# A graph layer's gathers and sums: loads moved to ScalarE's queue, one-hot tiles built earlier, three PSUM buffers for sums, and empty steps behind a pack's stores

## The chip, the cores and the metric

The kernel runs on one core of a Trainium2 chip. The metric is the device time of one launch in microseconds (us); a kernel's time is the median of several runs. One execution is also taken by the profiler, and everything that is said of lines, waits and engines comes from that one.

The core has TensorE (PE in the profile; PEld is its loading of weights), VectorE (DVE), ScalarE (ACT), GpSimd (POOL) and SyncE (SP). Each has its own queue and takes its instructions in order; they wait for one another through semaphores. SP does nothing here but issue DMAs, and ScalarE and GpSimd can issue them as well.

## What is computed

A graph layer on 50,000 nodes of 160 numbers and 1,650,000 edges, sorted by destination. Each edge sends a message that is linear in its source's row and in the edge's four numbers; the messages are added up by destination, go through another linear map and a relu, are added to x twice, and a layer norm over the 160 numbers ends it.

```python
s = x[:, :MUL0]
v = x[:, MUL0:].reshape(n, MUL1, 3)
ss, vv = (s[src], v[src])
e0 = sh[:, 0:1]
e1 = sh[:, 1:4]
dot = jnp.einsum('eui,ei->eu', vv, e1)
out0 = C0 * (ss * e0 @ W1 + dot * INV3 @ W2)
p3 = (ss @ W3)[:, :, None] * e1[:, None, :] * INV3
p4 = jnp.einsum('eui,uw->ewi', vv * e0[:, :, None], W4) * INV3
p5 = jnp.einsum('eui,uw->ewi', jnp.cross(vv, e1[:, None, :]), W5) * INV6
out1 = C1 * (p3 + p4 + p5)
m = jnp.concatenate([out0, out1.reshape(-1, 3 * MUL1)], axis=1)
m_agg = jax.ops.segment_sum(m, dst, num_segments=n)
hs = m_agg[:, :MUL0] @ Ws * LIN_S
hv = jnp.einsum('nui,uw->nwi', m_agg[:, MUL0:].reshape(n, MUL1, 3), Wv) * LIN_V
h = jnp.concatenate([hs, hv.reshape(n, 3 * MUL1)], axis=1)
...
x = _layernorm(x + x + jax.nn.relu(h), axis=-1)
```

(The last line puts together what two functions of the reference do.)

## The kernel before

The order of the two linear steps is turned round: the kernel first adds up, for each node, the gathered rows weighted by each of the edge's four numbers (4 x 160 sums per node), and then multiplies these sums by one matrix that joins all the weights.

**Edges.** A unit is 128 edges, a group is 6 units whose destinations lie in 32 neighbouring nodes, and a *pair* is two groups: 12 units. There are 1,044 pairs, and the main loop (line 853) runs over them. For a pair p:

- `gather` (L345): 12 indirect DMAs on GpSimd (L349), each bringing 128 rows of x (640 bytes apiece) into the tile `xg`. That pool (`rows`) has 4 buffers, so the first gather of pair p waits for the last matmul of pair p-4.
- `spread` (L354), on VectorE: `hot` (L358) is 1 where an edge's destination is one of the 32 nodes, and `ha` (L361) is `hot` times the edge's four numbers, 128 columns per unit.
- `group_sums` (L381): 12 matmuls on TensorE (L386), `ha` against `xg`, into `ps`, a PSUM tile of 2 x 160 columns from a pool of 2 buffers (`psA`). They are fp32 and run in two passes, so the profile has 25,044 of them. It is a generator that gives control back after each matmul.
- `turn_sums` (L394), on VectorE: a transpose of `ps` into `sums` (L398) and two additions into the `ring` (L405), the running sums of a stretch of nodes.

**Nodes.** 391 blocks of 128 nodes. When no later group touches a block, tasks are put into a queue that `work` (L748) draws from after each of the 12 matmuls of a pair: `do_ahead` (the load of `xt`, rows of x for two blocks, L644), 2 pairs later `do_block` (five matmuls of the ring with the joined weights into `phb`, L704, then `y`, `st` and `mv` on VectorE, L182 to L186), 3 pairs later `do_root` (`rstd` by ScalarE, L191), 4 pairs later `do_store` (reciprocal L195 and `o` L196 on VectorE), 6 pairs later `do_send` (`out`, L784, for two blocks). `phb` comes from the pool `psM` of 2 buffers.

**Edges' data.** Every 10 pairs `load` (L250) brings the next 20 groups' indices and numbers; `do_place` makes the tiles of indices (`si`), of places (`rel`) and of the edges' numbers (`pk`, in PSUM) from it, starting with `first` on VectorE (L318) and a small matmul into `bank` (L320). A first part of the edges is read as it is. The rest is first packed by the kernel itself: each node's edge to itself is taken out of the lists, the rest closed up.

**Packs.** 16 packs of 128 long rows of edges, one after another, each over some 63 pairs. `pack` (L463) gives a list of steps, some of them empty (`None`): a read (L474 to L478), 59 steps of work on ScalarE and VectorE (L482 to L584) and empty ones, then 17 `store` steps, in each of which SP issues up to 16 DMAs to places that it reads from a table (L618): a row of `edges` and a row of `selves` for each of 8 rows. The loop (L872 to L881) spreads the steps evenly over the pairs between one pack's end and the next one's due pair. `load` then reads `edges`, and `ask_own` (L661) reads `selves` (`sr`) and the rows of x (`xr`, L675) for two blocks at a time, 6 pairs before their segment's first pair; `set_own` puts them into the ring.

**Queues.** SP issues all loads, all results and all stores, in program order: `dq = nc.sync`. ScalarE computes `rstd` and the packs' casts and issues a few loads at the start. GpSimd issues only gathers. The order within each queue is the program's order (a manual schedule, L851). The order of TensorE's and VectorE's work in a pair is set by the j at which the loop does things:

```python
for j, ps in enumerate(group_sums(p, rows, has.pop(p))):
    if j == 1 and turning:
        turn_sums(*turning)
        turning = None
    if j == 3 and p + 1 < len(pairs):
        s1, g1, ng1 = pairs[p + 1]
        has[p + 1] = spread(placed[s1], (g1 - s1 * SG) * G, ng1 * G)
    work(1.0)
```

`turning` is the pair before, so VectorE turns pair p-1 and then builds `ha` of pair p+1.

Of the kernel before, what the change touches and what calls it, by code (L numbers as in the profile page):

```python
# [50 lines left out]
P = 128  # L51
# [22 lines left out]
RP = 128  # L74
RS = 16
KM = 31

def plan(n_nodes, n_edges):

# [23 lines left out]
def tile_gnn_resnorm(ctx: ExitStack, tc: tile.TileContext, x, src, dst, attr, W1, W2, W3, W4, W5, Ws, Wv, out, n_edges):  # L103
# [123 lines left out]
    with tc.tile_pool(name="once", bufs=1) as once, tc.tile_pool(name="raw", bufs=2) as rawp, \  # L227
# [2 lines left out]
            tc.tile_pool(name="ring", bufs=2) as ringp, tc.tile_pool(name="node", bufs=3) as np_, \  # L230
            tc.tile_pool(name="ahead", bufs=4) as aheadp, tc.tile_pool(name="outs", bufs=3) as outp, \
            tc.tile_pool(name="psC", bufs=1, space=PSUM) as psC, tc.tile_pool(name="psK", bufs=2, space=PSUM) as psK, \
            tc.tile_pool(name="psP", bufs=1, space=PSUM) as psP, tc.tile_pool(name="psA", bufs=2, space=PSUM) as psA, \
            tc.tile_pool(name="psM", bufs=2, space=PSUM) as psM, ExitStack() as later_pools:

        spotp, ownp = (later_pools.enter_context(tc.tile_pool(name=name, bufs=bufs))
                       for name, bufs in (("spot", 3), ("own", 2)))
# [6 lines left out]
        slotsP = bank[:, 0, :]  # L244
        nc.vector.tensor_copy(slotsP, slots)

        dq = nc.sync
        begun = []

        def load(s):  # L250

            g0 = s * SG
            n = (min(NG, g0 + SG) - g0) * G
            if g0 >= NH:
                p0 = g0 * G * P - EH
                r6 = rawp.tile([P, P, 2 + NK], F32, name="r6")
                dq.dma_start(r6[:n].rearrange("u p c -> u (p c)"),
                             edges[0, p0 * (2 + NK):(p0 + n * P) * (2 + NK)].rearrange("(u q) -> u q", u=n))
                return s, n, None, r6[:n, :, 0], r6[:n, :, 1], r6[:n, :, 2:]
            e = slice(g0 * G * P, (g0 * G + n) * P)  # L260
            ri = rawp.tile([P, 2, P], I32, name="ri")
            ra = rawp.tile([P, P, NK], F32, name="ra")
            dq.dma_start(ri[:n, 0, :], src1[e].rearrange("(u p) o -> u (p o)", p=P))
            dq.dma_start(ri[:n, 1, :], dst1[e].rearrange("(u p) o -> u (p o)", p=P))
            dq.dma_start(ra[:n].rearrange("u p k -> u (p k)"), attr[e].rearrange("(u p) k -> u (p k)", p=P))
            return s, n, ri, None, None, ra[:n]

        def cast(loaded):
# [102 lines left out]
        def fresh(kind):  # L371
            written[kind].append([])

        def wrote(kind, ins):
            ws = written[kind]
            for old in ws[-3] if len(ws) > 2 else []:
                tc.declare_no_dep(ins.ins, old, reason="its reader has waited for it")
            ws[-1].append(ins.ins)
            return ins

        def group_sums(p, rows, ha):  # L381

            ps = psA.tile([P, PG, D], F32, name="ps")
            fresh("ps")
            for j, xr in enumerate(rows):
                mm = nc.tensor.matmul(ps[:, j // G, :], ha[:, j].rearrange("p k w -> p (k w)"), xr,  # L386
                                      start=j % G == 0, stop=j % G == G - 1)
                if j % G == 0:
                    wrote("ps", mm)
                else:  # L390
                    written["ps"][-1].append(mm.ins)
                yield ps
# [70 lines left out]
        def pack(c):  # L463
# [7 lines left out]
            def read():  # L471
                T["pri"] = pri = packp.tile([P, 2, L + 1], I32, name="pri")
                T["pra"] = pra = packp.tile([P, LW, NK], F32, name="pra")
                dq.dma_start(pri[:n, 0, :L], src1[e].rearrange("(r e) o -> r (e o)", e=L))  # L474
                dq.dma_start(pri[:n, 1, :L], dst1[e].rearrange("(r e) o -> r (e o)", e=L))

                dq.dma_start(pri[:n, 1, L:], dst1[e0 + L:e0 + L + n * L].rearrange("(r e) o -> r (e o)", e=L)[:, 0:1])
                dq.dma_start(pra[:n, :L].rearrange("r e k -> r (e k)"), attr[e].rearrange("(r e) k -> r (e k)", e=L))  # L478

            def begin():  # L480
                T["prow"] = rows = packp.tile([P, L + 1, C], F32, name="prow")
# [142 lines left out]


            for head, j in [(False, j) for j in range(RS)] + [(True, 0)]:
                steps.append(partial(store, head, j))
            return steps + [stored]

        def rows_of(b):  # L630
            nb = min(P, N - b * P)
# [2 lines left out]
        def together(b):  # L634

            bs = list(range(b // BP * BP, min(nblocks, b // BP * BP + BP)))
            return bs if all(rows_of(i)[0] == P for i in bs) else [b]

        def ahead(bs):

            nb = rows_of(bs[0])[0]
            n0, n1 = rows_of(bs[0])[1].start, rows_of(bs[-1])[1].stop
            xt = aheadp.tile([P, BP, D], F32, name="xt")
            dq.dma_start(xt[:nb, :len(bs)], x[n0:n1, :].rearrange("(h n) d -> n h d", h=len(bs)))  # L644

            return [(xt[:, h],) for h in range(len(bs))]

# [13 lines left out]
        def ask_own(k, bs, got):  # L661

            n0, n1 = rows_of(bs[0])[1].start, rows_of(bs[-1])[1].stop
            assert rows_stored[0] == NR or row_start(rows_stored[0])[1][0] >= n1
            n = n1 - n0
            nq = next(q for q in range(math.ceil(n / W), n + 1) if n % q == 0)
            m = n // nq
            assert nq <= BP * P // W
            xr = ownp.tile([P, BP * P // W, D], F32, name="xr")
            sr = ownp.tile([P, BP * P // W], F32, name="sr")  # L670
            xs = x[n0:n1, :].rearrange("(w q) d -> w (q d)", q=nq).unsqueeze(0).to_broadcast([NK, m, nq * D])
            ss = selves[0, n0 * NK:n1 * NK].rearrange("(w q k) -> k w q", q=nq, k=NK)
            with nc.allow_non_contiguous_dma(reason="one number of each node"):
                if m == W:
                    dq.dma_start(xr[:, :nq].rearrange("p q d -> p (q d)"), xs)  # L675
                    dq.dma_start(sr[:, :nq], ss)
                else:
                    nc.vector.memset(xr[:, :nq], 0.0)
                    nc.vector.memset(sr[:, :nq], 0.0)
                    for k_ in range(NK):  # L680
                        r = slice(k_ * W, k_ * W + m)
                        dq.dma_start(xr[r, :nq].rearrange("p q d -> p (q d)"), xs[k_])
                        dq.dma_start(sr[r, :nq], ss[k_])
            got.extend((xr, sr, nq))

        def set_own(k, bs, got):
# [8 lines left out]
            if c0 + nq * W < c1:  # L695
                nc.vector.memset(ring[k][:, :, c0 + nq * W:c1], 0.0)

        def block(b, xt):
            nb, row = rows_of(b)
            k, c0 = b // SB, b % SB * P  # L700
            ph = psM.tile([P, D], F32, name="phb", tag="misc")
            fresh("misc")
            for i in range(ND):
                wrote("misc", nc.tensor.matmul(ph[:nb], ring[k][:, i, c0:c0 + nb], BWk[:, i, :],  # L704
                                               start=i == 0, stop=i == ND - 1))
                yield 1
            return norm1(np_, ph[:nb], xt[:nb], nb)
# [33 lines left out]
        def after_pair(p, f, *args):  # L741
            later.setdefault(p, []).append((f, args))
# [15 lines left out]
                else:  # L758
                    credit[0] -= cost

        of_nodes, resid, rstds, outs = {}, {}, {}, {}

        def do_ahead(b):
            bs = together(b)
# [1 line left out]
                of_nodes.update(zip(bs, ahead(bs)))  # L766

        def do_block(b):
            resid[b] = yield from block(b, *of_nodes.pop(b))

        def do_root(b):
            rstds[b] = norm2(np_, resid[b][1], rows_of(b)[0])
# [7 lines left out]
        def do_send(b):  # L780
            bs = together(b)
            if b == bs[-1]:
                n0, n1 = rows_of(bs[0])[1].start, rows_of(b)[1].stop
                dq.dma_start(out[n0:n1, :].rearrange("(h n) d -> n h d", h=len(bs)),  # L784
                             outs.pop(bs[0])[:rows_of(b)[0], :len(bs)])

        def do_cast(s):
# [57 lines left out]
                after_pair(p - 2, set_own, k, bs, got)  # L845
        for b, g in enumerate(last_of):
            p = g // PG
            after_pair(max(p, START - 1), do_ahead, b)
            for d, f in ((2, do_block), (3, do_root), (4, do_store), (6, do_send)):
                after_pair(p + d, f, b)  # L850
        later_pools.enter_context(tc.manual_schedule(engines={ET.SP, ET.PE, ET.DVE, ET.Activation}))  # L851
        turning = None
        for p, (s, g, ng) in enumerate(pairs):
# [8 lines left out]
                    after_pair(p + 8, read_flags)  # L862
            rows = gather(placed[s], (g - s * SG) * G, ng * G)
            for j, ps in enumerate(group_sums(p, rows, has.pop(p))):
                if j == 1 and turning:
                    turn_sums(*turning)
                    turning = None
                if j == 3 and p + 1 < len(pairs):
                    s1, g1, ng1 = pairs[p + 1]
                    has[p + 1] = spread(placed[s1], (g1 - s1 * SG) * G, ng1 * G)  # L870
                work(1.0)
                if packs and p >= START:  # L872
                    when = p + (j + 1) / (ng * G)
                    todo = math.ceil(len(packs[0]) * min(1, (when - began) / max(1, due[0] - began)))
                    for step in packs[0][done:todo]:
                        if step:
                            step()
                    done = max(done, todo)
                    if done == len(packs[0]):
                        packs.pop(0), due.pop(0)  # L880
                        done, began = 0, when  # L881
# [174 lines left out]
```

## Time and profile before

| what | value |
|---|---|
| median of 10 runs | 17,998.04 us (17,987.92 to 18,016.4) |
| the profiled execution: time of the run | 17,988.15 us |
| its span in the profile | 17,986.0 us |
| TensorE's granted clock, mean | 0.625 |
| DMA traffic | 1,337 MB, 74 GB/s over the span |
| gathers' share of the 16 DMA engines' time | 24.2% |
| one gather on GpSimd (L349), shortest / median / longest | 940 / 946 / 4,777 ns |
| transposes of `sums` (L398) | 529.3 us busy, 5,996.5 us idle before them |
| `y` (L182) | 125.7 us busy, 3,784.8 us idle before |
| additions into the ring (L405) | 683.0 us busy |

Busy time is the time in which an engine runs instructions; issuing DMAs, waiting on semaphores and branches don't count. "Idle before" is the time that an engine did nothing just ahead of the instructions of a line, with what ended it; "remote" there means a releaser that the trace doesn't show, and "issue" means that nothing was waited for as far as the profile shows. In the list of waits a line reads: engine and line, what it waited for, total, number of times, longest.

### The profile page before, as it was taken

The numbers are of one execution on the slowest core, as the hardware profiler recorded it, in microseconds if no ns is written. First come the engines' busy times: TensorE is split into PE (matmuls) and PEld (weight loads), VectorE is DVE, ScalarE is ACT, GpSimd is POOL, SyncE is SP. The second block draws the span as 40 slices with busy tenths as digits, with TensorE's granted clock in tenths as the row PEclk, the third lists the DMA queues.
The fourth block names the chain that finished last, engine by engine and source line by source line (L and its number), as shares of the span: only waits on it lengthen the run. The fifth ranks groups of instructions, "written<-read, shape, count | busy, mean of one in ns | idle before, by whom it ended". The sixth has DMA issues, their size and how long they took to land. (4 is left out here: it accounts for less than half of the span.)

```text
span 17986.0 us, 99721 instructions
## 1 busy us (share of the span) xinstructions
PE 6903.9 (38%) x29811; PEld 6018.3 (33%) x29812; DVE 7033.1 (39%) x11269; ACT 228.2 (1%) x479; POOL 12110.3 (67%) x12535
## 2 busy tenths in 40 slices
PE   3333333333333333333333333334333333334334
PEld 3333333333333333333333333333333333333333
DVE  4343443434434343443433434344343433434332
ACT  0000000000000000000000000000000000000000
POOL 6666666666666666666666666666666666666666
PEclk6666666666666666666666666666666666666666
DMA  2222323233232322323223233332323223233322
GB/s 71 75 69 72 80 70 81 69 81 72 71 81 70 83 69 73 80 69 83 72 71 80 70 79 73 79 73 72 81 70 82 69 73 80 69 81 72 73 72 63
DMA packets 961715, 1337.18 MB, mean 74 GB/s; under 512 B 411739, under 2 KB 716048, under 8 KB 957182
## 3 DMA queue, kind: packets, MB, share of 16 engines
q0 software_dynamic: 601056, 1026.60, 24.2%
q1 hardware_dynamic: 358674, 302.87, 6.1%
q8 instruction: 238, 3.90, 0.1%
q14 instruction: 307, 2.51, 0.0%
q10 hardware_dynamic: 1440, 1.29, 0.0%
HBM read 1258.50 MB, written 71.40 MB: 74 GB/s over the span
## 5 line engine op out<-in xcount | busy, mean ns | idle before, releaser
L349 POOL DMA_INDIRECT xg<-in_x,si x12522 | 12106.6, 967 | 5854.0 <-issue 3663.0
L386 PE MATMUL ps<-xg,ha 128*128 128x160 f32 x25044 | 6279.1, 383 | 9065.1 <-issue 8170.0
L386 PEld LDWEIGHTS ps<-xg,ha 128*128 128x128 f32 x25044 | 5181.9, 254 | 9865.6 <-issue 8903.4
L398 DVE STREAM_TRANSPOSE sums<-ps 128x320 f32<-128x320 f32 x1044 | 529.3, 507 | 5996.5 <-remote 3768.2
L361 DVE TENSOR_TENSOR ha<-hot,pk 128x1536 f32<-128x1536 f32 x1044 | 1830.4, 1753 | 35.8
L182 DVE SCALAR_TENSOR_TENSOR y<-phb,xt 128x160 f32<-128x160 f32 x391 | 125.7, 321 | 3784.8 <-PE ps L386 1817.9
L704 PE MATMUL phb<-BWk,ring 128*128 128x160 f32 (+1 forms) x3910 | 1177.8, 386 | 464.1 <-issue 462.7
L704 PEld LDWEIGHTS phb<-BWk,ring 128*128 128x128 f32 (+1 forms) x3910 | 917.0, 263 | 477.4 <-issue 476.6
L405 DVE TENSOR_TENSOR ring<-ring,sums 128x160 f32 x2087 | 683.0, 327 | 310.5 <-issue 220.1
L358 DVE TENSOR_TENSOR hot<-bank,rel 128x384 f32<-128x384 f32 x1044 | 572.8, 549 | 137.8 <-remote 91.6
L693 DVE STREAM_TRANSPOSE ring<-xr 128x1280 f32<-128x1280 f32 x188 | 465.9, 2478 | 6.5
L566 DVE COPY_PREDICATED prow<-marks,prow 128x2370 f32<-128x2370 int32 (+8 forms) x160 | 445.3, 2783 | 1.1
L320 PE MATMUL bank<-first,ones 120*128 120x20 f32 (+1 forms) x210 | 57.8, 357 | 769.6 <-DVE first L318 506.0
L191 ACT ACTIVATE rstd<-mv,eps_t 128x1 f32<-128x1 f32 x391 | 115.2, 295 | 17028.1 <-DVE st L184 5280.4
L320 PEld LDWEIGHTS bank<-first,ones 120*128 120x128 f32 (+1 forms) x210 | 49.0, 287 | 808.0 <-DVE first L318 529.0
L326 PE MATMUL bank<-ident,r 120*128 120x120 f32 x100 | 46.5, 465 | 702.8 <-DVE baseB L322 401.1
L566 DVE COPY_PREDICATED pra<-marks,pra 128x1580 f32<-128x1580 int32 (+8 forms) x160 | 306.8, 1917 | 0.0
L689 DVE TENSOR_TENSOR xr<-xr,sr 128x1280 f32<-128x1280 f32 x188 | 277.0, 1474 | 57.1 <-DMA sr<-selves 32.7
L326 PEld LDWEIGHTS bank<-ident,r 120*128 120x128 f32 x100 | 21.1, 211 | 727.0 <-DVE baseB L322 414.9
L196 DVE TENSOR_SCALAR o<-y,mv,rstd 128x160 f32<-128x160 f32 x391 | 147.3, 377 | 18.9 <-remote 2.9
L402 DVE TENSOR_TENSOR ring<-ring 128x1280 f32<-128x1280 f32 x97 | 142.8, 1473 | 1.8
L331 PE MATMUL pk<-ident,r 120*128 120x120 f32 (+1 forms) x400 | 140.0, 401 | 0.0
(349 smaller groups left out, 2157.5 us busy)
## 6 DMA issues: line engine op xcount, KB each, us to landing
xg<-in_x,si POOLq DMA_INDIRECT x12522
xr<-in_x SPq DMA_DIRECT2D x187, 640.0 KB
edges<-prow SPq DMA_DIRECT2D x1994, 18.5 KB
r<-edges SPq DMA_DIRECT2D x99, 360.0 KB
selves<-mine SPq DMA_DIRECT2D x1992, 0.5 KB
xt<-in_x SPq DMA_DIRECT2D x195, 160.0 KB
out<-o SPq DMA_DIRECT2D x195, 160.0 KB
pra<-in_attr SPq DMA_DIRECT2D x15, 1580.0 KB
```

The lines of the kernel that those rows point to most:

```text
L196: nc.vector.tensor_scalar(o[:n], y[:n], mv[:n, 0:1], rstd[:n], op0=ALU.subtract, op1=ALU.mult)
L349: nc.gpsimd.indirect_dma_start(out=xg[:, j, :], out_offset=None, in_=x, in_offset=bass.IndirectOffsetOnAxis(ap=placed[0][:, u + j:u + j + ...
L358: nc.vector.tensor_tensor(hot[:, :n], slotsP[:, 0:W].unsqueeze(1).to_broadcast([P, n, W]), rel[:, u:u + n].unsqueeze(2).to_broadcast([P, n ...
L361: nc.vector.tensor_tensor(ha[:, :n], hot[:, :n].unsqueeze(2).to_broadcast([P, n, NK, W]), pk[:, :, u:u + n].rearrange("p k u -> p u k").un ...
L386: mm = nc.tensor.matmul(ps[:, j // G, :], ha[:, j].rearrange("p k w -> p (k w)"), xr, start=j % G == 0, stop=j % G == G - 1)
L398: nc.vector.transpose(at[:, :ng], ps[:, :ng].rearrange("p g (b f) -> p g b f", f=FB))
L402: nc.vector.tensor_tensor(ring[k][:, :, :TW - S], ring[k][:, :, :TW - S], ring[k - 1][:, :, S:], op=ALU.add)
L405: nc.vector.tensor_tensor(here, here, at[:, i], op=ALU.add)
L566: nc.vector.copy_predicated(what[:n, a:e], mi[:, r].unsqueeze(2).to_broadcast([n, e - a, what.shape[2]]), what[:n, a + d:e + d])
L689: nc.vector.tensor_tensor(xr[:, :nq], xr[:, :nq], sr[:, :nq].unsqueeze(2).to_broadcast([P, nq, D]), op=ALU.mult)
L693: nc.vector.transpose(ring[k][:, :, c0:c0 + nq * W].rearrange("p b (w q) -> p q b w", q=nq), xr[:, :nq].rearrange("p q (b f) -> p q b f", ...
L704: wrote("misc", nc.tensor.matmul(ph[:nb], ring[k][:, i, c0:c0 + nb], BWk[:, i, :], start=i == 0, stop=i == ND - 1))
```

## The change

- `load` (but for the very first), the packs' reads, `xt`, `xr` and `sr`, and the results `out` are issued by ScalarE (`loads = nc.scalar`). The stores stay on SP.
- `xt` is asked for 3 pairs earlier.
- `ha` of pair p+1 is built at j == 0, ahead of the turn of pair p-1, which stays at j == 1.
- The pool of `ps` has 3 buffers, that of `phb` one, whose tile holds two blocks and is taken at the first of the two. `wrote` declares away the order between a `ps` tile's matmuls and those of the tile whose buffer it takes over, now the fourth last; for the others nothing is declared any more.
- In a pack each store step is followed by an empty one, and the end of the pack by 70 empty ones: 164 steps, where there were 77, spread over the same pairs.

```diff
+REST = 70
...
-            tc.tile_pool(name="psP", bufs=1, space=PSUM) as psP, tc.tile_pool(name="psA", bufs=2, space=PSUM) as psA, \
-            tc.tile_pool(name="psM", bufs=2, space=PSUM) as psM, ExitStack() as later_pools:
+            tc.tile_pool(name="psP", bufs=1, space=PSUM) as psP, tc.tile_pool(name="psA", bufs=3, space=PSUM) as psA, \
+            tc.tile_pool(name="psM", bufs=1, space=PSUM) as psM, ExitStack() as later_pools:
...
-        dq = nc.sync
+        dq, loads = nc.sync, nc.scalar
...
         def load(s):
 
+            q = loads if s else dq
...
-                dq.dma_start(r6[:n].rearrange("u p c -> u (p c)"),
+                q.dma_start(r6[:n].rearrange("u p c -> u (p c)"),
...
         def wrote(kind, ins):
             ws = written[kind]
-            for old in ws[-3] if len(ws) > 2 else []:
+            for old in ws[-4] if kind == "ps" and len(ws) > 3 else []:
                 tc.declare_no_dep(ins.ins, old, reason="its reader has waited for it")
...
-                dq.dma_start(pri[:n, 0, :L], src1[e].rearrange("(r e) o -> r (e o)", e=L))
+                loads.dma_start(pri[:n, 0, :L], src1[e].rearrange("(r e) o -> r (e o)", e=L))
...
             for head, j in [(False, j) for j in range(RS)] + [(True, 0)]:
-                steps.append(partial(store, head, j))
-            return steps + [stored]
+                steps += [partial(store, head, j), None]
+            return steps + [stored] + [None] * REST
...
-            dq.dma_start(xt[:nb, :len(bs)], x[n0:n1, :].rearrange("(h n) d -> n h d", h=len(bs)))
+            loads.dma_start(xt[:nb, :len(bs)], x[n0:n1, :].rearrange("(h n) d -> n h d", h=len(bs)))
...
-                    dq.dma_start(xr[:, :nq].rearrange("p q d -> p (q d)"), xs)
-                    dq.dma_start(sr[:, :nq], ss)
+                    loads.dma_start(xr[:, :nq].rearrange("p q d -> p (q d)"), xs)
+                    loads.dma_start(sr[:, :nq], ss)
...
-        def block(b, xt):
+        def block(b, xt, ph):
             nb, row = rows_of(b)
             k, c0 = b // SB, b % SB * P
-            ph = psM.tile([P, D], F32, name="phb", tag="misc")
-            fresh("misc")
...
         def do_block(b):
-            resid[b] = yield from block(b, *of_nodes.pop(b))
+            bs = together(b)
+            if b == bs[0]:
+                sums_of[b] = psM.tile([P, BP, D], F32, name="phb", tag="misc")
+                fresh("misc")
+            resid[b] = yield from block(b, *of_nodes.pop(b), sums_of[bs[0]][:, b - bs[0]])
...
-                dq.dma_start(out[n0:n1, :].rearrange("(h n) d -> n h d", h=len(bs)),
+                loads.dma_start(out[n0:n1, :].rearrange("(h n) d -> n h d", h=len(bs)),
                              outs.pop(bs[0])[:rows_of(b)[0], :len(bs)])
...
-            after_pair(max(p, START - 1), do_ahead, b)
+            after_pair(max(p - 3, START - 1), do_ahead, b)
...
             for j, ps in enumerate(group_sums(p, rows, has.pop(p))):
+                if j == 0 and p + 1 < len(pairs):
+                    s1, g1, ng1 = pairs[p + 1]
+                    has[p + 1] = spread(placed[s1], (g1 - s1 * SG) * G, ng1 * G)
                 if j == 1 and turning:
                     turn_sums(*turning)
                     turning = None
-                if j == 3 and p + 1 < len(pairs):
-                    s1, g1, ng1 = pairs[p + 1]
-                    has[p + 1] = spread(placed[s1], (g1 - s1 * SG) * G, ng1 * G)
                 work(1.0)
```

More of the change, by code (lines that the diff above doesn't have):

```diff
@@ L262, in load @@
             ra = rawp.tile([P, P, NK], F32, name="ra")
-            dq.dma_start(ri[:n, 0, :], src1[e].rearrange("(u p) o -> u (p o)", p=P))
-            dq.dma_start(ri[:n, 1, :], dst1[e].rearrange("(u p) o -> u (p o)", p=P))
-            dq.dma_start(ra[:n].rearrange("u p k -> u (p k)"), attr[e].rearrange("(u p) k -> u (p k)", p=P))
+            q.dma_start(ri[:n, 0, :], src1[e].rearrange("(u p) o -> u (p o)", p=P))
+            q.dma_start(ri[:n, 1, :], dst1[e].rearrange("(u p) o -> u (p o)", p=P))
+            q.dma_start(ra[:n].rearrange("u p k -> u (p k)"), attr[e].rearrange("(u p) k -> u (p k)", p=P))
             return s, n, ri, None, None, ra[:n]
@@ L473, in read @@
                 T["pra"] = pra = packp.tile([P, LW, NK], F32, name="pra")
-                dq.dma_start(pri[:n, 0, :L], src1[e].rearrange("(r e) o -> r (e o)", e=L))
-                dq.dma_start(pri[:n, 1, :L], dst1[e].rearrange("(r e) o -> r (e o)", e=L))
-                dq.dma_start(pri[:n, 1, L:], dst1[e0 + L:e0 + L + n * L].rearrange("(r e) o -> r (e o)", e=L)[:, 0:1])
-                dq.dma_start(pra[:n, :L].rearrange("r e k -> r (e k)"), attr[e].rearrange("(r e) k -> r (e k)", e=L))
+                loads.dma_start(pri[:n, 0, :L], src1[e].rearrange("(r e) o -> r (e o)", e=L))
+                loads.dma_start(pri[:n, 1, :L], dst1[e].rearrange("(r e) o -> r (e o)", e=L))
+                loads.dma_start(pri[:n, 1, L:], dst1[e0 + L:e0 + L + n * L].rearrange("(r e) o -> r (e o)", e=L)[:, 0:1])
+                loads.dma_start(pra[:n, :L].rearrange("r e k -> r (e k)"), attr[e].rearrange("(r e) k -> r (e k)", e=L))
             def begin():
@@ L681, in ask_own @@
                         r = slice(k_ * W, k_ * W + m)
-                        dq.dma_start(xr[r, :nq].rearrange("p q d -> p (q d)"), xs[k_])
-                        dq.dma_start(sr[r, :nq], ss[k_])
+                        loads.dma_start(xr[r, :nq].rearrange("p q d -> p (q d)"), xs[k_])
+                        loads.dma_start(sr[r, :nq], ss[k_])
             got.extend((xr, sr, nq))
@@ L759, in work @@
                     credit[0] -= cost
-        of_nodes, resid, rstds, outs = {}, {}, {}, {}
+        of_nodes, resid, rstds, outs, sums_of = {}, {}, {}, {}, {}
         def do_ahead(b):
```

## The prediction

> **What bounds the kernel now.** I read the engines' busy times first, then the list of waits, then the groups of instructions, then one stretch of the timeline. The waits of GpSimd (POOL):
>
> ```profile
> span 17986.0 us, 99721 instructions
> PE 6903.9 (38%) x29811; PEld 6018.3 (33%) x29812; DVE 7033.1 (39%) x11269; ACT 228.2 (1%) x479; POOL 12110.3 (67%) x12535
> ...
> POOL xg L349 <- issue: 3663.0, 12005, 1.8
> POOL xg L349 <- PE ps L386: 1176.2, 224, 46.8
> POOL xg L349 <- remote: 929.2, 231, 7.7
> POOL xg L349 <- PE phb L704: 63.9, 11, 7.6
> ```
>
> The columns of the last four lines are total idle us, times, longest. GpSimd issues 12,522 gathers. They are busy 12,106.6 us (third block below) and 3,663.0 us lie between them as issue, 0.305 us apiece, for which nothing else is to blame. Its whole idle time before L349 is 5,854.0, so 5,854.0 - 3,663.0 = 2,191 us are real waits, nearly all of them for TensorE to free a gather buffer (the three rows above are 2,169 us in 466 waits, 4.65 us each). 12,106.6 + 3,663.0 + 2,191 = 17,961, and some 25 us of start and tail make the span. No other engine is over 39% busy. So the floor of this kernel is near 15,800 us (17,986 - 2,191), and everything turns on the 2,191.
>
> Why is TensorE late? The rows of the groups, and the other engines' waits:
>
> ```profile
> L349 POOL DMA_INDIRECT xg<-in_x,si x12522 | 12106.6, 967 | 5854.0 <-issue 3663.0
> L386 PE MATMUL ps<-xg,ha 128*128 128x160 f32 x25044 | 6279.1, 383 | 9065.1 <-issue 8170.0
> L361 DVE TENSOR_TENSOR ha<-hot,pk 128x1536 f32<-128x1536 f32 x1044 | 1830.4, 1753 | 35.8
> ...
> DVE sums L398 <- remote: 3768.2, 278, 42.1
> DVE y L182 <- PE ps L386: 1817.9, 129, 34.5
> DVE y L182 <- DMA xt<-in_x: 233.5, 7, 93.3
> ```
>
> L386 is idle 9,065 us and 8,170 of them are "issue": the profile sees nothing that it waits for. The timeline shows it; start, duration, then idle time before in brackets:
>
> ```profile
> 9002.57 0.42 PE L386 MATMUL ps<-xg,ha 128*128 128x160 f32 x1 [2.38 <-issue]
> 9005.37 0.43 PE L386 MATMUL ps<-xg,ha 128*128 128x160 f32 x1 [2.37 <-issue]
> 9008.17 0.43 PE L386 MATMUL ps<-xg,ha 128*128 128x160 f32 x1 [2.37 <-issue]
> 9010.99 0.32 DVE L182 SCALAR_TENSOR_TENSOR y<-phb,xt 128x160 f32<-128x160 f32 x1 [30.14 <-PE ps L386]
> 9012.20 0.94 POOL L349 DMA_INDIRECT xg<-in_x,si  x1 [6.04 <-PE ps L386]
> 9018.02 5.97 PE L386 MATMUL ps<-xg,ha 128*128 128x160 f32 x24 [4.33 <-issue]
> ```
>
> TensorE creeps, one half-matmul (fp32 takes two) each 2.8 us, until GpSimd has stood still for some microseconds; then VectorE's wait ends too, and TensorE does 24 in 5.97 us. About half of the span (9,186 us in 358 stretches) is such creeping. I counted from the trace's instruction times what goes with it. At the start of 331 of 419 stalls of GpSimd over 1 us, TensorE was creeping (its last matmul under 3 us before); at 88 it stood. A stall's mean length by the pairs of groups since the last stall is 3.64 us (1 pair), 4.46 (2), 5.92 (3), 6.16 (4): about 2 us per pair, however the stalls fall. So something passes TensorE's instructions at a nearly fixed rate while gathers are issued, and a stall is where it catches up. Of what nature it is the trace doesn't tell.
>
> **The change, part by part.**
>
> *Loads and results to ScalarE.* Some 950 DMA issues leave SP for ScalarE, 228.2 us busy. At 0.4 to 0.7 us each (timeline: `out` 0.40, `xt` 0.46) that is 400 to 650 us on an idle engine; on the path they cost nothing. What they save is waiting behind SP's stores: 17 store steps per pack of 16 stores each. The 93.3 us above is `xt` queued behind pack 0's stores; VectorE, then TensorE, then GpSimd stood, the 46.8 us. Only one other long stall leads to a late load: 10.0 us at 10,652, a pack's read that came late (ScalarE 54.7 us on `pri`, VectorE 33.1 behind it). Seven near 11.5 us have another cause (TensorE stands at the group start L320 for VectorE's `first`, which stands behind `y`, which waits for TensorE's notice), and the change leaves that order alone. Gain: (46.8 - 4.65) + (10.0 - 4.65) = 47 us. Bounds: 0, if new waits take their place, to 94, if every stall above 8 us falls back to 4.65 (nine, 136 us in all, less 9 x 4.65). I take 47. `xt` (195 issues), asked for 3 pairs earlier, is in the same sum.
>
> The Trainium skill ("Trainium Kernel Development and Optimization", Key Constraints) speaks against this part: queues of several engines run on the same DMA engines, so splitting them saves only the issuing engine's time. By it alone the part is worth 0. The profile has 233.5 us of waits for `xt`, which were issue order, not transfer.
>
> What is now queued behind them: `rstd` (L191) on ScalarE, and behind it the reciprocal (L195) at the head of VectorE's queue. The second `xr` issue of a segment held SP 12 to 18 us (15.66 at 813.55). The cover: ScalarE waits for `st`, `mv`, `y` 14,363 us in all (44.5 us of it in this stretch of the timeline), so these issues mostly end before VectorE reaches the block. `out` waits for `o` there too, but the `rstd` behind it needs still later work of VectorE. The cover is thin: `rstd` was ready 15.2 us (median) before the reciprocal, under 8 in a quarter of 391 cases. Taken at 0; priced in rival B.
>
> *`ha` before the turn.* No instruction is added; hot and ha (0.549 + 1.753 us) now stand before the turn of pair p-1, not behind it. In before a turn that waits for TensorE's notice holds back the next `ha`, for which TensorE then waits. I counted 43 stalls that begin in that state, 5.6 us each. Bounds: 0 (the 2 us per pair are only paid later) to 43 x 5.6 = 240 us. Between: the stall comes one pair later, at 3.5 pairs rather than 2.5. By the lengths above that is (4.46 + 5.92)/2 / 2.5 = 2.08 against (5.92 + 6.16)/2 / 3.5 = 1.73 us per pair, over 43 x 3.5 = 150 pairs: 53 us. I take 53, since the rows by length speak for it.
>
> *Three buffers for `ps`, one for `phb` (for two blocks).* TensorE's first matmul of a pair now needs the turn of p-3, not p-2. While it creeps, no buffer holds it, so I take 0; the upper bound is in rival A. The Trainium skill ("Perfetto Trace Analysis", Optimizing Strategies) would have independent groups change PSUM banks so that reading out overlaps matmuls; by it this gains what TensorE waits for `ps`, which the 331 of 419 above leave small. With one `phb` the first matmul of the next two blocks waits for `y`: in before `y` ended 22 us (median) ahead of the next block's first matmul, and later than it in 2 of 390. 0 to 2 x 7 = 14 us lost; I take 0.
>
> *Empty steps.* A pack's 77 steps become 164 over the same time (some 63 pairs), stores every second step. Stores keep their spacing (63/77 = 0.82 pair, then 2 x 63/164 = 0.77); VectorE's pack work falls into a third of the time, not 0.7. VectorE is 39% busy; at most some 2,150 us of that is pack work (what 7,033 leaves above turns, hot, ha, ring, blocks), 134 us a pack, so 134/(0.34 x 63) = 6.3 us per pair in that third instead of 3.0, with 17.2 us (17,986/1,044) to a pair. The idle 61% hides it. If it didn't: 16 packs x 21 pairs x 3.3 = 1,100 us, the far end. The stalls of before are as frequent in stretches with pack work as in those with stores, so I take 0. That the stores end 27 pairs earlier means that `prow`'s copies and the loads of stored edges find them landed.
>
> *Sum.* 17,986.0 - 47 - 53 = 17,886. The run of this profile took 17,988.15 (2 more than the span), the median of ten is 17,998.04, 10 above it: 17,886 + 12 = 17,898; say 17,900 (-0.54%).
>
> **Rivals.**
>
> A, much faster. TensorE's "issue" time is hidden waiting for VectorE, and the two edits that part them let it run at its fast rate. For: 24 half-matmuls in 5.97 us, so a pair needs 6 of 17.2 us; VectorE waits 5,996 us before L398. Against: in the creeping lines `ha` was done and the gathers landed. All 2,169 us gone would be 15,830; a third gone, which I think the middle of this case, 17,998 - 723 = 17,275.
>
> B, slower. ScalarE sits in an `xr` issue of 15.5 us when `mv` comes; the reciprocal stops VectorE, TensorE wants `ha`, GpSimd its buffer. Price by the mutual waits above: 11.5 - 4.65 = 6.9 us each, 95 such issues, 655 us at most: 17,898 + 655 = 18,553. It decides over the gains from 100/6.9 = 15 of the 95 on; half of them give 17,898 + 328 = 18,226.
>
> C, nothing. New waits (ScalarE's issues share their semaphores with SP's stores) eat the 47, and the fixed 2 us per pair the 53: 17,990.
>
> **How the numbers follow.** The forecast 0.45 (its own range 17,800 to 17,960), A 0.15, B 0.22, C 0.18. About 0.2%, 36 us, is what a measurement of this kernel can tell from no change: 17,962 to 18,034. Faster: all of A, 0.42 of the forecast's 0.45 and 0.01 of C: 0.58. Same: 0.03 of the forecast, most of C, a little of B: 0.20. Slower: the rest of B and C, 0.22. For 8 in 10 I leave out the deeper half of A (below 17,400) and the worse half of B (above 18,230).
>
> **What would show it.** Right: the 46.8 us stall and `y <- DMA xt` gone; GpSimd's waits near 2,090 us, still some 2 us per pair; L386's "issue" still near 8,000; the gathers' 967 ns unchanged. Wrong: "issue" on L386 falls by thousands (A); VectorE idle before L195, released by `rstd`, over 300 us (B); GpSimd's waits unchanged in sum (C). If the creeping depends on what ScalarE issues, the 2 us per pair will move, and nothing here prices that.

## The result, and the profile after

The changed kernel takes 18,974.51 us (median of 8 runs, 18,948.88 to 19,000.14) against 18,000.66 us of the kernel before beside it (28 runs): a ratio of 1.054, 95% interval 1.053 to 1.0549, 974 us slower. The forecast was 17,900, the range up to 18,230. The kernel before itself took 17,993 to 18,108 us beside this run and beside e1 to e4 and e9 to e12, but 15,969 to 15,999 us beside e5 to e8 and e13 to e18, so each run is compared only with the runs of the kernel before that were taken beside it.

The first block is from the page of the changed kernel (its span, then groups: busy time and mean ns, then idle time before and what ended most of it), the second from its list of waits (total us, times, longest).

```profile
span 18975.3 us, 99815 instructions
...
L351 POOL DMA_INDIRECT xg<-in_x,si x12522 | 12128.4, 969 | 6822.6 <-issue 3688.3
L388 PE MATMUL ps<-xg,ha 128*128 128x160 f32 x25044 | 6286.0, 377 | 9083.1 <-issue 8220.5
...
L505 DVE TENSOR_TENSOR hit<-marks,prow 128x395 f32<-128x395 f32 (+1 forms) x32 | 27.0, 842 | 1686.0 <-ACT marks L504 1674.1
```

```profile
POOL xg L351 <- PE ps L388: 2289.4, 230, 92.2
...
DVE hit L505 <- ACT marks L504: 1674.1, 27, 148.4
...
ACT prow L484 <- DMA edges<-prow: 1449.0, 15, 162.8
```

GpSimd's idle time grew by 6,822.6 - 5,854.0 = 969 us, nearly all of the 989 us by which the two profiled spans differ; its gathers cost much the same (969 ns, before 967, 22 us in all). The longest wait was 46.8 us and is now 92.2. Listed one by one, 15 of GpSimd's waits last 63 to 92 us, 1,155 us together, one at the beginning of each pack's work but the first; all others make 1,979. The last two rows of the second block name the chain: VectorE stands at `hit` (the first work of a pack) for ScalarE's `marks`, and ScalarE stood at `prow` for stores of the *previous* pack, 116 to 163 us in ten of the 15 packs. In the other five it had stood for those stores already at the `rstd` just ahead, 156 to 170 us, and only some 5 us are left at `prow`. `prow` has one buffer, and the stores read it. The kernel before had next to nothing of this:

```profile
ACT prow L482 <- DMA edges<-prow: 44.8, 1, 44.8
...
DVE hit L503 <- ACT marks L502: 39.2, 4, 33.1
```

Those stores should have been done 27 pairs, some 470 us, earlier. SP's own list of waits shows what held them, behind 3,181 us in which it waited for the pack's own data (its first row):

```profile
SPq L620 <- DVE prow L568: 3180.7, 11, 327.6
...
SPq L620 <- DMA xt<-in_x: 545.0, 12, 107.6
SPq L620 <- DMA sr<-selves: 398.7, 11, 144.6
SPq L620 <- DMA xr<-in_x: 386.2, 10, 94.9
SPq L620 <- DMA out<-o: 292.2, 7, 110.6
```

A store has nothing to do with `xt` or `out`, which ScalarE now issues. What they share are the semaphores of completion. In this trace the same eight serve 4,241 DMAs of SP and 964 of ScalarE (14 of ScalarE's in the kernel before), handed out in turn, and each DMA waits for the semaphore that it will use itself, that is until the DMA that had it before has landed. The turn can be read from the stores' semaphores: at first one to twelve stores of a pack follow each other before a DMA of ScalarE's comes between, but near the pack's end stands an unbroken run of 196 to 245 of the 272. So these can't start until the loads of the pack's last pairs have been issued, and those stand in ScalarE's queue behind `rstd`. One such end of a pack, from the timeline of the changed kernel (start, duration, idle time before in brackets):

```profile
2902.36 0.23 SPq L620 DMA_DIRECT2D selves<-mine  x1
...
3058.92 0.35 ACTq L259 DMA_DIRECT2D r<-edges  x1
...
3063.59 0.23 SPq L620 DMA_DIRECT2D selves<-mine  x1
3064.60 1.58 ACT L484 CAST prow<-pri 128x790 f32<-128x790 int32 x1 [137.72 <-DMA edges<-prow]
...
3070.71 0.84 DVE L505 TENSOR_TENSOR hit<-marks,prow 128x395 f32<-128x395 f32 x1 [134.04 <-ACT marks L504]
...
3076.33 6.32 PE L388 MATMUL ps<-xg,ha 128*128 128x160 f32 x24 [109.65 <-issue]
...
3082.91 0.94 POOL L351 DMA_INDIRECT xg<-in_x,si  x1 [87.40 <-PE ps L388]
```

The store at 2,902 uses the semaphore of an `xr` load that ScalarE had issued only at 2,877, behind an `rstd`; SP has its last store out at 3,063.6. (A load of ScalarE's, `r`, is held in turn until 3,058.9 by semaphores that stores had before it.) One microsecond after the last store ScalarE casts `prow`, 6 us after that VectorE goes on at `hit`, behind which `ha` stands in its queue, then TensorE, then GpSimd. Each link is shorter than the one before: 138, 134, 110, 87 us, as the tiles that were ready ahead last for a while.

### The profile page after: what moved, and what is told of

It reads as the page before. It is cut to its first block, busy times and chain, and to the rows that moved or that the text cites. A ratio compares the mean times of both kernels' runs of the same rounds, so it can differ in the third digit from the quotient of the medians.

```text
span 18975.3 us, 99815 instructions
## 1 busy us (share of the span) xinstructions
PE 7030.3 (37%) x29811; PEld 5911.0 (31%) x29812; DVE 7039.0 (37%) x11269; ACT 224.6 (1%) x479; POOL 12132.1 (64%) x12535
## 5 line engine op out<-in xcount | busy, mean ns | idle before, releaser
L351 POOL DMA_INDIRECT xg<-in_x,si x12522 | 12128.4, 969 | 6822.6 <-issue 3688.3
L388 PEld LDWEIGHTS ps<-xg,ha 128*128 128x128 f32 x25044 | 5062.6, 247 | 10005.7 <-issue 9204.3
```

The source lines that it names most:

```text
L351: nc.gpsimd.indirect_dma_start(out=xg[:, j, :], out_offset=None, in_=x, in_offset=bass.IndirectOffsetOnAxis(ap=placed[0][:, u + j:u + j + ...
```

## The experiments

The theories: S, the stores are held back by the shared semaphores; D, VectorE's work on the packs, twice as dense, is late; Q, `rstd` is late behind the loads in ScalarE's queue; P, a term of the prediction; F, a fixed rate of TensorE's instructions.

**e1: where the stores stand, and nothing else.** An order without a semaphore (`NoSync`) puts each step's stores ahead of the next pair's first matmul when the semaphores are handed out.

```diff
+                while placed_early:
+                    tc.add_manual_dep(mm.ins, placed_early.pop().name,
+                                      mybir.DependencyInfo(mybir.DependencyClass.NoSync, mybir.DependencyReason.DATA),
+                                      reason="place in the order")
...
+                placed_early.append(dq.dma_start(mem[ds(at, size)].rearrange("(o f) -> o f", o=1),
+                                                 what.bitcast(U8).rearrange("p e c -> p (e c)")).ins)
```

> The changed kernel, with one order added that costs no semaphore: the stores of a step are placed ahead of the next pair's first matmul when semaphores are handed out, so that they share them with the loads of their own pairs and not with those of the pack's end. Theory S (in the changed kernel most stores of a pack stand, in the order in which the shared completion semaphores are handed out, right ahead of the next pack's prow; ScalarE waits there for SP, VectorE for ScalarE's marks, TensorE for VectorE, GpSimd for TensorE, 15 times 63 to 92 us): 17,850 to 17,960 us, no wait of GpSimd over 20 us after the first pack, ScalarE's wait of prow for edges 1,449 us to under 150, VectorE's of hit for marks 1,674 to under 300. Theory D (VectorE's pack work, twice as dense, is what is late): 18,950 to 19,000, the waits for marks unchanged. Theory Q (loads and results ahead of rstd in ScalarE's queue): above 18,700, since that queue is unchanged.

18,013.11 us, 1.0006 of before (0.9996 to 1.0015): the loss is gone with every engine's own order unchanged. The rows `hit` for `marks` and `prow` for `edges` are no longer among the 60 largest waits, and in its trace no store falls within the 200 us ahead of a `prow` (18 do ahead of the second pack's), where the changed kernel has 205 to 221 of 272 in each pack from the third on. SP's waits for `xr`, `out` and `sr` fall from 1,077 us to 86, and those for `xt` are gone. S is shown; D and Q, which expected 18,700 and more, fall as the cause of the loss. But 18,013 is not in the 17,850 to 17,960 that S expected, nor 17,900. Its waits:

```profile
POOL xg L351 <- PE ps L389: 1191.5, 214, 27.8
POOL xg L351 <- remote: 836.9, 190, 9.9
...
DVE rstd L196 <- issue: 699.0, 27, 74.8
...
ACT rstd L192 <- DMA selves<-mine: 573.6, 9, 108.2
ACT rstd L192 <- DMA edges<-prow: 570.4, 7, 120.9
...
DVE rstd L196 <- ACT rstd L192: 378.9, 10, 67.1
```

ScalarE's `rstd` now waits behind loads that wait for SP's stores, and VectorE stands at the reciprocal (L196), 379 us of it for `rstd` and 699 us under "issue": rival B's place, from another cause. The longest wait of GpSimd is 27.8 us.

**e2: loads and results back on SP**, the rest of the change kept (`dq, loads = nc.sync, nc.sync`).

> The changed kernel with loads and results issued by SP again (all else of the change stays). Theory S: SP's own order keeps the stores ahead of the loads that follow them, and nothing of ScalarE's is waited for: 17,880 to 18,020, the 15 waits of GpSimd over 60 us gone. Theory D: 18,900 to 19,000, as the steps of the packs are unchanged. Theory Q: 17,880 to 18,020 too.

18,015.11 us, 1.0006 (0.9997 to 1.0016). D falls here too: the packs' steps are as dense as in the changed kernel. S and Q both allow this time.

**e3 and e4: without the empty steps; the loads alone.** e3 is the changed kernel with a pack's 77 steps of before, e4 the kernel before with `q`, `loads` and `nc.scalar` as in the change and nothing else.

> The changed kernel without the empty steps (77 steps in a pack, as before). Theory S: about 240 of a pack's some 250 stores still stand right ahead of prow, so the waits of 63 to 92 us stay or grow: 18,900 to 19,150. Theory D: 17,880 to 17,990. Theory Q: 18,900 to 19,000.

> The kernel before with one part of the change alone: loads and results issued by ScalarE. Theory S: 15 long waits of GpSimd at the packs' ends: 18,900 to 19,150. Theory D: 17,930 to 18,010 (no empty steps, so no denser work). Theory Q: 18,900 to 19,150 too, but with VectorE waiting at the reciprocal for rstd, over 300 us, where S has it waiting at hit for marks.

e3 19,042.39 us, 1.0581 (1.0563 to 1.0599); e4 19,069.5, 1.0593 (1.0575 to 1.0611). Moving the loads alone costs 1,076 us, more than the whole change; the empty steps don't cause the loss but give back some of it (1.058 of before without them, 1.054 with them). Waits of e4:

```profile
DVE rstd L195 <- ACT rstd L191: 1305.0, 12, 133.7
...
ACT rstd L191 <- DMA edges<-prow: 845.0, 5, 173.6
...
ACT prow L483 <- DMA edges<-prow: 598.0, 14, 193.5
DVE hit L504 <- ACT marks L503: 427.0, 16, 120.3
```

In e4 VectorE stands mostly at the reciprocal, as Q says, and less at `hit`; so Q had this sign right. But what ScalarE's `rstd` waits for there is the same as `prow` in the changed kernel, SP's stores, and GpSimd's 15 waits over 60 us are there too (1,218 us). That the steps decide which of the two comes first in VectorE's queue is a reading of the rows, not tried.

**e5 to e8: single parts, and a pause.** All four fell where the kernel before took 15,970.93 us. e5 moves the block of `spread` to j == 0; e6 has the pools of `ps` and `phb` and `do_block` as in the change; e7 has `max(p - 3, START - 1)` for `do_ahead`; e8 adds ten small memsets of GpSimd behind each pair's gathers:

```diff
+            with tc.issue_after(last.ins):
+                for _ in range(10):
+                    idled.append(nc.gpsimd.memset(idle, 0.0).ins)
```

> The kernel before with ha built ahead of the turn (j == 0), and nothing else of the change. Theory P (the prediction's term): 53 us less, 17,935 to 17,955, the stalls that begin with TensorE standing at a pair's first matmul fewer than 43 and GpSimd's real waits (2,191) at most 2,150. Theory F (something passes TensorE's instructions at a fixed rate, some 17.2 us per pair, whatever stands ahead of it): within 25 us of before, the waits between 2,150 and 2,230.

> The kernel before with three buffers of ps and one of phb for two blocks, and nothing else. Theory P (taken at 0) and theory F: within 25 us of before. Rival (VectorE's turn holds TensorE, so a third buffer frees it): over 150 us less, L386's idle time by issue, 8,170, down by over 500.

> The kernel before with xt asked for 3 pairs earlier (still on SP), and nothing else. Theory P: the 46.8 us stall and the 233.5 us of waits of y for xt go, 25 to 50 us less: 17,945 to 17,975. Theory F: the stall goes, the sum of the waits of GpSimd stays within 40 us (what is saved once is waited later): within 25 us of before.

> The kernel before with ten small memsets of GpSimd (some 2 us together) behind each pair's 12 gathers, work that nobody needs. Theory F (a fixed rate; GpSimd's stalls are only where it waits for it): the pauses replace stalls, 17,950 to 18,250, GpSimd's waits down from 2,191 to under 600. Theory C (a stall is a price of its own, paid for each catching up, and comes on top): 1,044 x 2 = 2,090 more, 19,900 to 20,200.

e5 15,965.15 (0.9996, 0.9987 to 1.0005), e6 15,970.22 (0.9999, 0.999 to 1.0008), e7 15,969.12 (0.9998, 0.9989 to 1.0007), e8 18,797.15 (1.177). None of them tests its theory: there is nothing to remove. No profile of the kernel before was taken beside them; the page of e7, whose time is the same, stands for it:

```profile
L349 POOL DMA_INDIRECT xg<-in_x,si x12522 | 12153.2, 971 | 3826.2 <-issue 3535.5
L386 PE MATMUL ps<-xg,ha 128*128 128x160 f32 x25044 | 9960.7, 509 | 5267.5 <-DMA xg<-in_x,si 5121.0
```

The gathers are the same (971 ns), but TensorE waits for them to land, not for "issue": it doesn't creep, GpSimd has only 291 us of idle time besides issue, and 2 waits over 1 us (before: 419). The floor that the prediction worked out, 15,800 us, is nearly met. e8 adds 2,826 us, 2.7 per pair.

**e9 to e12: again, beside a kernel before that took 18,107.75 us.** e9 is the changed kernel, e10 is e5, e11 is e8, e12 the kernel before with the empty steps alone.

> The changed kernel once more, since the kernel before took 17,993 us beside the first four experiments and 15,971 beside the next four (without the creeping of TensorE). Where before takes about 18,000 here: 18,950 to 19,000. Where it takes about 15,970: theory S' (the 213 stores ahead of prow cost what SP takes for them; SP creeps as TensorE does, and without the creeping the stores take 0.26 us each, 55 us, which the four pairs of gathered rows cover): 15,950 to 16,150. Theory S'' (the order of the semaphores alone costs 72 us a pack, whatever SP's rate): 16,900 to 17,100.

> The kernel before with ha ahead of the turn alone, as in e5. Where before takes about 15,970, within 25 us of it as in e5. Where it takes about 18,000: theory P 17,935 to 17,965; theory F within 25 us.

> The kernel before with ten small memsets of GpSimd behind each pair's gathers, as in e8, where they cost 2.7 us per pair. Where before takes about 18,000: theory F (fixed rate, the pauses replace stalls) 18,780 to 19,100; theory C (stalls come on top) 20,600 to 20,900. Where before takes about 15,970: 18,780 to 18,820 as in e8.

> The kernel before with the 87 empty steps of a pack (its work twice as dense, its stores followed by 70 empty steps), loads still on SP. Theory S: within 40 us of before in either case, as all stores and loads are in SP's own order. Theory D: 100 us or more above it.

e9 19,090.18 us, 1.0539 (1.0522 to 1.0555): as at first. e10 18,060.05, 0.9974 (0.9965 to 0.9983), 48 us less: P's 53 us are there in size, and F in its strict form, that nothing ahead matters, falls. That they come in the way the prediction says isn't shown: e10's real waits of GpSimd are 2,277 us, above the 2,191 of the first profile, and beside 18,108 us none of the kernel before was taken. e11 18,797.12, the time of e8 to the microsecond, though before stands 2,137 us higher. Its waits, and the memsets' group:

```profile
POOL xg L354 <- PE ps L394: 471.6, 875, 0.9
...
L359 POOL MEMSET idle<- 1x128 f32 x10440 | 2043.0, 196 | 539.6
```

No wait for TensorE exceeds 0.9 us: a pause of 2.7 us per pair took the place of all stalls, and the creeping is gone with them. C (stalls on top, 20,600) falls. This takes e11 to have met the same condition as the runs beside it, which all crept; had it alone met the other one, it would have taken e8's 18,797 us as well, and no run rules that out. e12 18,221.46, 1.0066 (1.005 to 1.0081): 114 us more, so D has a part here. GpSimd's waits over 8 us exceed 4.65 us each by 212 us in all, against 93 in before, and `y` waits 441.0 us for `xt` against 233.5. That late loads are the cause is argued from these rows, not tried.

**e13 to e18: shorter pauses, combinations, and the changed kernel without creeping.** e13 and e18 have two memsets, e14 five, e15 joins e5 and e7, e16 is e6, e17 the changed kernel. All fell where before took 15,969 to 15,999 us.

> The kernel before with two small memsets of GpSimd behind each pair's gathers (0.27 us each by e8 and e11, where ten of them took the place of every stall). Where before takes about 18,000: theory F (a fixed rate, some 17.2 us per pair; pauses only take the place of stalls) 17,950 to 18,150, GpSimd's real waits about 1,630; theory L (TensorE creeps only once it has fallen behind, and a short breath keeps it from falling behind) 16,500 to 16,650, waits under 200. Where before takes about 15,970: 16,500 to 16,600.

> The same with five memsets (1.35 us per pair). Where before takes about 18,000: theory F 17,950 to 18,150, waits about 800; theory L 17,350 to 17,500. Where before takes about 15,970: 17,350 to 17,450.

> The kernel before with ha ahead of the turn and xt asked for 3 pairs earlier, all loads on SP. Where before takes about 18,000: theory P 0.9945 to 0.998 of before (48 us as in e10, and up to 42 for the stall of 46.8); theory F no better than e10 beyond its interval's other end, 0.997 to 1.000. Where it takes about 15,970: within 25 us.

> The kernel before with three buffers of ps and one of phb alone, as in e6. Where before takes about 18,000: theories P and F 0.998 to 1.002 of before; if VectorE's turn holds TensorE there, 0.99 or less. Where it takes about 15,970: within 25 us, as in e6.

> The changed kernel beside whichever state this run falls in. Where before takes about 15,990: theory S' (SP doesn't creep, so the stores ahead of prow cost 55 us or so a pack, covered by four pairs of gathered rows) 15,970 to 16,150; theory S'' (72 us a pack whatever SP's rate) 16,900 to 17,150. Where before takes about 18,000: 1.053 to 1.055 of it, as twice.

> The kernel before with two small memsets behind each pair's gathers, as in e13, where they cost 745 us and before had no stalls to take the place of. Where before takes about 18,000: theory F (a fixed rate, pauses take the place of stalls) 17,950 to 18,150; theory L (a short breath keeps TensorE from falling behind) 16,700 to 16,800, which is faster than before. Where before takes about 15,990: 16,735 to 16,755.

e13 16,744.22 and e18 16,714.81 (1.0466 and 1.0468), e14 17,520.88 (1.0951), e15 15,986.37 (0.9993, 0.9984 to 1.0002), e16 15,999.15 (1.0, 0.9991 to 1.0009). The pauses of e13 and e14 cost more than their texts expected (16,500 to 16,600 and 17,350 to 17,450). Whether a pause shorter than 2.7 us would avoid the creeping, and so beat the kernel before where that takes 18,000, stays open, as do the terms for `xt` and for the third `ps` buffer there. No version beat the kernel before in both conditions; ha ahead of the turn alone beat it where TensorE creeps and was the same where it doesn't.

e17 is the telling one: 16,023.16 us against 15,969.22, 1.0032 (1.002 to 1.0045). The same program, with the same order of semaphores, loses 54 us here and 974 there. Its waits:

```profile
POOL xg L351 <- PE ps L388: 246.0, 584, 19.3
...
DVE hit L505 <- ACT marks L504: 1049.3, 32, 92.9
...
ACT prow L484 <- DMA edges<-prow: 702.9, 12, 109.2
```

The chain is still there, up to VectorE. But the last 200 stores ahead of `prow` take 95 to 100 us, not 116 to 165: here they lie 0.32 us apart (median) while GpSimd gathers, in the first trace 0.72 us while it gathers and 0.32 while it stands. And TensorE comes to the wait with next to nothing left undone, 0.2 pairs behind GpSimd (median at the start of a pair's gathers), where the creeping one is 1.8 behind. GpSimd's longest wait for TensorE is 19.3 us. That its four pairs of rows cover the rest is read from the two traces, not tried one by one. S' was right in that the loss goes, wrong in the size of the stores (55 us expected).

## Why the prediction was wrong, point by point

- **Loads and results to ScalarE, "on the path they cost nothing", gain 47.** This is the step that failed. Moved alone, they cost 1,076 us (e4). I looked at what the moved DMAs cost and at what is queued behind them on ScalarE, but not at what SP's stores would wait for once ScalarE issued 964 of the 5,205 DMAs that share their semaphores. I named the sharing in rival C and priced it at the 47 us of the gain; its price is a pack's worth of stores, 15 times some 72 us (77 less the usual 4.65), where TensorE and SP creep, and 54 us for the whole change where they don't (e17). No rival's end came near: the highest was B's 18,553. (Of the nine stalls above 8 us, 135 us in all and not 136, one of the "seven near 11.5" lasts 8.5; nothing rests on it.)
- **Empty steps, "`prow`'s copies and the loads of stored edges find them landed".** Wrong in the same way: a step's place in the list says what SP issues next, not when. I read 0.36 to 0.57 of the pack's period from the list; in the trace the last stores come 1 us before `prow`. Taken alone on SP (e12) I had the empty steps at 0 of a possible 1,100; they cost 114.
- **`ha` before the turn, 53 us.** Right in size where TensorE creeps: 48 us (31 to 63, e10). Whether the stalls that the term counts are the ones that went isn't shown.
- **Three buffers of `ps`, one of `phb`, 0.** 0 where nothing creeps (e6, e16); not tried where it does. The rule that the prediction cites here stands in the Trainium skill, "Perfetto Trace Analysis", under "Matmuls"; following it gained nothing in e6 and e16.
- **Rival B.** Its place (VectorE at the reciprocal, late `rstd`) showed in e3, e4 and e1, with 1,549, 1,305 and 379 us, and not in the changed kernel. Its cause, `xr` issues of 15.5 us, wasn't it: the rows of e1 and e4 name SP's stores.
- **Rival A.** Without the creeping the kernel before takes 15,971 us; A had 15,830 as its end. But none of the change's edits brings that about.
- **"Some 2 us per pair, however the stalls fall".** True on the whole of the executions that creep (2,191 us over 1,044 pairs); but the prediction's own rows give 3.64 us for one pair and 6.16 / 4 = 1.54 per pair for four, so it isn't a fixed rate, as e10 bears out. That the same program on other occasions has none of it could not be read from one profile.

e1 and e2 come close to a sum of single parts: -48 (e10) + 114 (e12) - 47 (`xt`) = +19, measured +20 and +22. That is no test: the 47 was never measured alone (only the 46.8 us stall is gone from both traces), e10 and e12 ran on another occasion, each of the two has an interval of some 18 us either way, and e1 has waits for `rstd` of its own.

## What to carry to other kernels

Before moving DMAs to another queue, ask which semaphores they share with those that stay: a store can be held by a load that it has nothing to do with, and two queues in order become one. Then look for the tile with one buffer that the held store still reads, and count from there how many engines stand behind its next writer. Where a profile shows stalls with no releaser ("issue"), run the kernel on another occasion before building on them.

## What the runs showed of the hardware that wasn't expected

- The same kernel has two times 13% apart, 15,971 and 18,000 us, each the same within 0.3% over all runs of one occasion (27 of one, 28 of the other). The same chip showed both, beside e1 to e4 and beside e5 to e8. TensorE's matmuls take longer in the shorter one (509 ns in e7's trace against 383 on the mean, at a granted clock of 0.57 against 0.62) and the gathers the same (971 and 967 ns). In the longer one TensorE's and SP's instructions pass at a crawl while GpSimd issues gathers: a half-matmul each 2.8 us at the start of the prediction's timeline, SP's stores 0.72 us apart and not 0.32. What brings one or the other about isn't known from these runs.
- One pause of 2.7 us behind each pair's gathers costs 2,826 us where nothing creeps (e8), but only 689 us beside a kernel before that creeps (e11), since the stalls go: both come to 18,797 us.
